# Left window columns weighted by TensorE's diagonals instead of ScalarE, and one block of a third pair added up wholly on TensorE from the eleventh head on

## The chip, the core and the metric

The kernel runs on one core of one Trainium2 chip, in one launch. The metric is the device time in microseconds of one execution; lower is better. The core's engines work side by side and meet only through semaphores: TensorE (PE) multiplies matrices into PSUM, VectorE (DVE) and ScalarE (ACT) work element by element, GpSimd (POOL) issues indirect transfers and small vector work, and SyncE (SP) issues the other transfers.

## The reference, cut to what matters

The input is an image of 4 x 32 x 32 x 384. Layer 0 is a deformable attention with 6 heads of 64 channels; a linear attention and a mixture of experts follow as layer 1. The change touches the attention of layer 0 alone:

```python
attn = jnp.einsum('bmhc,bnhc->bhmn', qh, k) * scale          # 1024 x 1024 per image and head
disp = (ref.reshape(1, n, 1, 2) - pos.reshape(Bq * G, 1, n, 2)) * 0.5
bias = _bilinear_sample(rpe_img, disp)                       # zero border, four neighbours
attn = jax.nn.softmax(attn + bias, axis=-1)
out = jnp.einsum('bhmn,bnhc->bmhc', attn, v).reshape(Bq, Hq, Wq, NC)
```

The bias of one key against all 32 x 32 queries is a 33 x 33 window of a table, interpolated with four weights: an upper and a lower row weight, then a left and a right column weight. With t the window after the row weights, bias[y, x] = w2 * t[y, x] + w3 * t[y, x + 1].

## The kernel before

The attention runs over 24 heads (4 images x 6), which the text counts from 0 to 23. A head has 1024 keys, in 8 blocks of 128, taken as 4 pairs of blocks. There are 96 pairs, numbered p = 4 * head + kp, so the "third pair" of a head is kp = 2. Within a pair the first block is e = 0, the second e = 1. A tile holds the keys of a block on 128 partitions and the 1024 queries along the row; score tiles for a pair are 128 x 2 x 1024.

For each pair these functions run, each on its engine:

- `fetch_windows` (L1168, POOL): one indirect transfer per block brings the 128 windows.
- `upper` (L1184, ScalarE) makes t from the window's upper rows with weight 0; `lower` (L1194, VectorE) adds the lower rows with weight 1. t is 32 rows of 33.
- `left` (L1202, ScalarE) makes o, the left 32 columns of t times weight 2.
- `scores` puts two products into one PSUM tile `ps` for the pair: keys times queries (L1221), and o brought in by a product with the identity (L1226). Each product is cut into 64-row halves, so that q-k products and o products sit on different quarters of the array. A pair has a first and a second half of this work (`step` 0 and 1). Between them stands `turn_over` (L1241): a tiny ScalarE copy of a token, which waits for the first half and which the second half waits for. There is one `ps` buffer, four PSUM banks: the next pair's products start when the last reader of this pair is done.
- `right` (L1252, VectorE), once per block: S = t's right columns times weight 3, plus `ps`.
- `running` (L1270, VectorE) keeps the maximum over the pairs of a head, 128 x 2 x 1024 at a time; after the fourth pair the two halves are joined (L1272). `highest` and `spread` reduce it over the partitions with TensorE transposes (L1282, L1286, L1298) and copy it out of PSUM (L1306, ScalarE).
- `minus` (L1311, VectorE) subtracts the maximum, `weights_of` (L1315, ScalarE) takes exp, `values` (L1329, L1338, TensorE) sums values and weights into PSUM; `out_of` (L1354, ScalarE) copies these sums out after the head's last pair.

A loop over g interleaves pairs at different stages: values of pair g-5, minus and exp of g-4, running maximum of g, scores of g+1, upper, lower and left of g+2, windows of g+4. The order on TensorE, ScalarE, VectorE and POOL is the order in which these calls are written, and each engine's queue is strictly in order. For a head's third pair the calls of one turn stand so: values part 0, scores first half, upper, running, token, values part 1, minus, exp, scores second half, left, right. Remaining work of layer 0 (`project`, L1429 and L1441, and late key and value pieces, L270 and L286) is tucked into fixed places of the loop.

The stage before (convolution, offsets, sampling of x by 6 indirect gathers a tile, L871, and multiplications with VectorE, L886 to L891) is ordered by a planner with costs and due times; the first windows, uppers and lowers of the attention are placed among its last instructions. Tiles come from pools with a set number of buffers; where a pool's memory was another tile's before, the first use waits for that tile's last.

Of the kernel before, what the change touches and what calls it, by code (L numbers as in the profile page):

```python
# [19 lines left out]
P = 128  # L20
# [139 lines left out]
def body(  # L160
# [953 lines left out]

    with tc.tile_pool(name="b_w", bufs=1) as bwp, tc.tile_pool(name="b_qkv", bufs=2) as bq, tc.tile_pool(
        name="b_win", bufs=4
    ) as bwin, tc.tile_pool(name="b_t", bufs=4) as bt, tc.tile_pool(name="b_o", bufs=2) as bo_, tc.tile_pool(
        name="b_s", bufs=6
    ) as bS, tc.tile_pool(name="b_m", bufs=2) as bm, tc.tile_pool(name="b_ao", bufs=1) as bao, tc.tile_pool(
        name="b_y", bufs=3  # L1120
# [2 lines left out]
        nc.sync.dma_start(wo, w_out.rearrange("(a p) d -> p a d", p=P))  # L1123
        bo = bwp.tile([P, NC], F32, tag="bo", name="bo")
        nc.sync.dma_start(bo, bc(b_out, 0, P))
        units = [(b, h) for b in range(B) for h in range(G)]
        ao = {}
        heads = {}
# [28 lines left out]


        wins, ts, os_, pss, Ss, turns = {}, {}, {}, {}, {}, {}
        qk, vs, ms, nms, pbss, pos, avs = {}, {}, {}, {}, {}, {}, {}  # L1160

        def fetch_windows(p):
# [35 lines left out]
        def left(p, e):  # L1198

            if p < NP:  # L1200
                o = bo_.tile([P, HI, WI], F32, tag="o", name=f"o{p}_{e}")
                nc.scalar.activation(o, ts[p, e][:, :, 0:WI], AF.Copy, scale=weight(p, e, 2))  # L1202
                os_[p, e] = o.rearrange("p y x -> p (y x)")

        def scores(p, step):


            if p >= NP:
                return
            i, kp = divmod(p, KP)  # L1210
            if step == 0:
                if kp == 0:
                    qk[i] = load_qk(units[i])
                pss[p] = bps.tile([P, 2, N], F32, tag="s", name=f"ps{p}")
            q, k = qk[i]
            ps = pss[p]
            e, d = 1 - step, step
            made = []
            for f in range(2):
                for r in range(2):  # L1220
                    made.append(nc.tensor.matmul(  # L1221
                        ps[HALF[1 - r], e, FULL[f]], k[HALF[r], 2 * kp + e, :], q[HALF[r], FULL[f]],
                        start=(step == 0), stop=(step == 1),
                    ))
                for r in range(2):
                    made.append(nc.tensor.matmul(  # L1226
                        ps[HALF[r], d, FULL[f]], ident[HALF[r], HALF[r]], os_[p, d][HALF[r], FULL[f]],
                        start=(step == 0), stop=(step == 1),
                    ))
            if step == 0:  # L1230
                turns[p] = made
            else:
                for i_ in made:
                    tc.add_manual_dep(i_.ins, turns[p].ins.name, SYNC, reason="second quarters")
                del turns[p]
# [10 lines left out]
        def right(p):  # L1246

            if p < NP:
                ps = pss.pop(p)
                st = bS.tile([P, 2, N], F32, tag="S", name=f"S{p}")  # L1250
                for e in range(2):
                    nc.vector.scalar_tensor_tensor(  # L1252
                        st[:, e, :].rearrange("p (y x) -> p y x", x=WI),
                        ts.pop((p, e))[:, :, 1:WIN],
                        weight(p, e, 3),
                        ps[:, e, :].rearrange("p (y x) -> p y x", x=WI),
                        ALU.mult,
                        ALU.add,
                    )
                    del os_[p, e]  # L1260
                Ss[p] = st

        def running(p):

            if p < NP:
                i, kp = divmod(p, KP)
                if kp == 1:
                    ms[i] = bm.tile([P, 2, N], F32, tag="m", bufs=1, name=f"m{i}")
                if kp:
                    nc.vector.tensor_tensor(ms[i], Ss[p - 1] if kp == 1 else ms[i], Ss[p], ALU.max)  # L1270
                if kp == KP - 1:
                    nc.vector.tensor_tensor(ms[i][:, 0, :], ms[i][:, 0, :], ms[i][:, 1, :], ALU.max)  # L1272
# [952 lines left out]
```

## Time and profile before

| what | value |
| --- | --- |
| median of 3 runs | 2853.95 us (2847.24 to 2855.77) |
| profiled execution, its own time | 2848.14 us |
| its span, first to last instruction | 2846.1 us |
| TensorE busy, whole span | 2585.0 us (91%) |
| VectorE busy | 1578.6 us (55%) |
| ScalarE busy | 1158.2 us (41%) |
| GpSimd busy | 853.3 us (30%) |
| L1202 (o), ScalarE | 192 instructions, 212.8 us, mean 1144 ns |
| L1226 (o by identity), TensorE | 1536 records, 376.6 us, mean 609 ns |
| L1252 (right), VectorE | 192 instructions, 236.9 us, mean 1275 ns |
| L1270 (running maximum), VectorE | 72 instructions, 172.1 us |
| mean granted TensorE clock | 0.969 |

The busy shares are means over stages with different limits; the attention loop takes about 404 to 1370 us. A row such as L1226 gives the line, engine and operation, what is written and read, how many, their busy time together (overlaps counted once) and the mean of one. Each matrix product of 32-bit numbers appears as two records. "Idle before" is the engine's idle time just before the instruction, and what ended it. In a timeline the columns are start (us), length (us), engine, line, operation, how many were merged, and the idle time.

### The profile page before, as it was taken

Reading aid. Unit: us, or ns where it says so; the run is one execution under the profiler, and the core shown is the slowest. Engines: PE = TensorE matmul, PEld = TensorE weight load, DVE = VectorE, ACT = ScalarE, POOL = GpSimd, SP = SyncE. Lnnn points to the kernel's source line nnn. Section 1 sums busy time; section 2 is a strip of 40 time slices with the busy share of each in tenths; the row PEclk is TensorE's granted clock in tenths of the full one; section 3 lists DMA queues with packets and bytes.
Section 4 is the critical chain, followed back from the end, with each engine's and each line's share of the span. In section 5 each row is a group of like instructions: output and inputs, shape, how many; then the busy total and the mean of one; then the engine's idle time right before and its main releaser. Section 6 shows DMA issues by size and latency. Waiting matters only on the chain. (4 is left out here: it accounts for less than half of the span.)

```text
span 2846.1 us, 33342 instructions
## 1 busy us (share of the span) xinstructions
PE 2585.0 (91%) x12731; PEld 1283.9 (45%) x12731; DVE 1578.6 (55%) x2349; ACT 1158.2 (41%) x1532; POOL 853.3 (30%) x776
## 2 busy tenths in 40 slices
PE   8899838898989988888799898999999999999999
PEld 5555512332333333233365554555555555555566
DVE  3888859999999999999656765000101011011011
ACT  5565536777667766676323322111111111111121
POOL 1668853232333333332112335211112111021121
PEclk9899969999999999999999999999999999999999
DMA  7934575454546555544121312622223434374371
GB/s 205 257 115 133 173 209 165 130 154 145 164 145 194 177 157 149 145 151 127 55 74 52 119 45 70 250 103 103 103 103 119 146 129 142 114 255 172 117 267 58
DMA packets 267899, 404.77 MB, mean 142 GB/s; under 512 B 134674, under 2 KB 207634, under 8 KB 267356
## 3 DMA queue, kind: packets, MB, share of 16 engines
q1 hardware_dynamic: 214912, 230.43, 25.6%
q0 software_dynamic: 52112, 172.15, 18.6%
q8 instruction: 100, 1.64, 0.2%
q14 instruction: 59, 0.48, 0.1%
q10 hardware_dynamic: 716, 0.07, 0.0%
HBM read 345.68 MB, written 70.06 MB: 146 GB/s over the span
## 5 line engine op out<-in xcount | busy, mean ns | idle before, releaser
L2072 PE MATMUL ph<-d_xT,w 128*128 128x512 f32 (+1 forms) x1152 | 484.1, 554 | 1.3 <-ACT h L2079 1.3
L2104 PE MATMUL acc<-w,h 128*128 128x384 f32 x1392 | 480.3, 486 | 0.0
L1168 POOL DMA_INDIRECT win<-table,widx x192 | 278.2, 1449 | 642.4 <-DVE t L1194 612.8
L1221 PE MATMUL ps<-q,k 64*64 64x512 f32 x1536 | 380.3, 608 | 91.6 <-DVE S L1252 43.4
L2079 ACT ACTIVATE h<-ph,b1c 128x512 f32<-128x512 f32 (+1 forms) x192 | 124.2, 647 | 776.2 <-PE ph L2072 761.7
L1226 PE MATMUL ps<-o,ident 64*64 64x512 f32 x1536 | 376.6, 609 | 9.4 <-ACT o L1202 9.4
L2104 PEld LDWEIGHTS acc<-w,h 128*128 128x128 f32 x1392 | 264.1, 190 | 208.5 <-issue 73.2
L2072 PEld LDWEIGHTS ph<-d_xT,w 128*128 128x128 f32 x1152 | 217.0, 191 | 196.3 <-issue 144.5
L871 POOL DMA_INDIRECT ga<-img,pidx x192 | 233.3, 1215 | 145.7 <-DVE gd L600 62.5
L2134 POOL DMA_INDIRECT out<-rows,ei x67 | 67.2, 1003 | 699.4 <-DVE rows L2131 690.5
L1315 ACT ACTIVATE S<-S 128x2048 f32<-128x2048 f32 x96 | 183.4, 1910 | 190.3 <-DVE S L1311 190.3
L1221 PEld LDWEIGHTS ps<-q,k 64*64 64x64 f32 x1536 | 98.8, 133 | 354.4 <-issue 211.3
L1722 DVE COPY d_xT<-e_tr 128x512 f32<-128x512 f32 (+2 forms) x75 | 36.6, 512 | 385.5 <-PE e_tr L1719 385.5
L1194 DVE SCALAR_TENSOR_TENSOR t<-win,bw,t 128x1056 f32<-128x1056 f32 x192 | 244.5, 1314 | 5.1 <-ACT t L1184 3.9
L1252 DVE SCALAR_TENSOR_TENSOR S<-t,bw,ps 128x1024 f32<-128x1024 f32 x192 | 236.9, 1275 | 17.4 <-PE ps L1226 14.3
L2123 DVE SCALAR_TENSOR_TENSOR rows<-b2r,en,rows 128x384 f32<-128x384 f32 x67 | 40.7, 618 | 361.3 <-DMA rows<-out,ei 311.1
L1184 ACT ACTIVATE t<-win,bw 128x1056 f32<-128x1056 f32 x192 | 218.1, 1168 | 40.3 <-DMA win<-table,widx 39.2
L1202 ACT ACTIVATE o<-t,bw 128x1024 f32<-128x1024 f32 x192 | 212.8, 1144 | 35.2 <-DVE t L1194 30.0
L1329 PE MATMUL po<-S,v 128*64 128x512 f32 x768 | 199.0, 642 | 24.4 <-ACT av L1354 13.9
L1311 DVE TENSOR_TENSOR S<-S,pbs 128x2048 f32<-128x2048 f32 x96 | 218.9, 2282 | 2.0 <-ACT pbs L1306 2.0
L2131 DVE SCALAR_TENSOR_TENSOR rows<-acc,en,rows 128x384 f32<-128x384 f32 x67 | 41.4, 618 | 217.6 <-PE acc L2104 215.7
L1270 DVE TENSOR_TENSOR m<-m,S 128x2048 f32<-128x2048 f32 x48 | 117.1, 2440 | 1.6
(350 smaller groups left out, 3441.8 us busy)
## 6 DMA issues: line engine op xcount, KB each, us to landing
w<-in_L_ffn_w SPq DMA_DIRECT2D x50, 2304.0 KB
img<-in_x SPq DMA_DIRECT2D x48, 256.0 KB
q<-q_d SPq DMA_DIRECT2D x48, 256.0 KB
x<-in_x SPq DMA_DIRECT2D x8, 768.0 KB
q_d<-qt SPq DMA_DIRECT2D x24, 256.0 KB
v_d<-qkvw SPq DMA_DIRECT2D x32, 192.0 KB
v<-v_d SPq DMA_DIRECT2D x24, 256.0 KB
k<-k_d SPq DMA_DIRECT2D x48, 128.0 KB
```

The costliest lines, as they stand in the source:

```text
L871: nc.gpsimd.indirect_dma_start(out=ga[:, g].rearrange("p s c -> p (s c)"), out_offset=None, in_=img[b][:, :], in_offset=bass.IndirectOffse ...
L1168: nc.gpsimd.indirect_dma_start(out=win, out_offset=None, in_=tables[h // 2][:, :], in_offset=bass.IndirectOffsetOnAxis(ap=widx[b][:, nb, h ...
L1184: nc.scalar.activation(t.rearrange("p y x -> p (y x)"), wins[p, e][:, : HI * WIN], AF.Copy, scale=weight(p, e, 0),)
L1194: nc.vector.scalar_tensor_tensor(tf, wins.pop((p, e))[:, WIN:], weight(p, e, 1), tf, ALU.mult, ALU.add)
L1202: nc.scalar.activation(o, ts[p, e][:, :, 0:WI], AF.Copy, scale=weight(p, e, 2))
L1221: made.append(nc.tensor.matmul(ps[HALF[1 - r], e, FULL[f]], k[HALF[r], 2 * kp + e, :], q[HALF[r], FULL[f]], start=(step == 0), stop=(step ...
L1226: made.append(nc.tensor.matmul(ps[HALF[r], d, FULL[f]], ident[HALF[r], HALF[r]], os_[p, d][HALF[r], FULL[f]], start=(step == 0), stop=(ste ...
L1252: nc.vector.scalar_tensor_tensor(st[:, e, :].rearrange("p (y x) -> p y x", x=WI), ts.pop((p, e))[:, :, 1:WIN], weight(p, e, 3), ps[:, e, : ...
L1311: nc.vector.tensor_tensor(Ss[p], Ss[p], bc(pbss[p // KP][:, :], 1, 2), ALU.add)
L1329: nc.tensor.matmul(pos[i][0][HALF[f], :], vs[i][:, 2 * kp + e, :], Ss[p][:, e, FULL[f]], start=(first and e == 0), stop=(last and e == 1),)
L2072: nc.tensor.matmul(ph if short(d) else ph[:, :n], a, m, start=(c == 0), stop=(c == CK - 1))
L2104: nc.tensor.matmul(d["acc"][0 if short(d) else s][:, :NC], h[:, s * P : (s + 1) * P], d["w2"][:, hc, :], start=(hc == 0), stop=(hc == HC - 1),
```

## The change

`left` no longer multiplies a block's columns. It makes a 128 x 64 tile: twice the 64 x 64 identity, stacked (`fold`, made once by two GpSimd copies), each row scaled with its key's weight 2. `scores` then multiplies with this diagonal instead of the identity, and moves the left columns of t itself, 16 rows of 32 out of 33, through TensorE.

For the second block of the third pair, in heads 10 to 23 (14 blocks), a second diagonal with weight 3 is made as well, and four further products in the second half of `scores` add the right columns of t to `ps`. `right` then leaves this block out; a ScalarE copy brings it from `ps` into S, and `running` takes the block's maximum out of `ps` directly and the other block's out of S, 128 x 1024 each, in place of one of 128 x 2048. The t pool goes from 4 to 5 buffers, the o pool from 2 to 6 of the smaller tiles.

```diff
@@ -1114,7 +1114,7 @@
 
     with tc.tile_pool(name="b_w", bufs=1) as bwp, tc.tile_pool(name="b_qkv", bufs=2) as bq, tc.tile_pool(
         name="b_win", bufs=4
-    ) as bwin, tc.tile_pool(name="b_t", bufs=4) as bt, tc.tile_pool(name="b_o", bufs=2) as bo_, tc.tile_pool(
+    ) as bwin, tc.tile_pool(name="b_t", bufs=5) as bt, tc.tile_pool(name="b_o", bufs=6) as bo_, tc.tile_pool(
         name="b_s", bufs=6
     ) as bS, tc.tile_pool(name="b_m", bufs=2) as bm, tc.tile_pool(name="b_ao", bufs=1) as bao, tc.tile_pool(
         name="b_y", bufs=3
@@ -1123,6 +1123,12 @@
         nc.sync.dma_start(wo, w_out.rearrange("(a p) d -> p a d", p=P))
         bo = bwp.tile([P, NC], F32, tag="bo", name="bo")
         nc.sync.dma_start(bo, bc(b_out, 0, P))
+
+        fold = bwp.tile([P, GC], F32, tag="fold", name="fold")
+        for e in range(2):
+            nc.gpsimd.tensor_copy(
+                fold[e * GC : (e + 1) * GC, :], ident[e * GC : (e + 1) * GC, e * GC : (e + 1) * GC]
+            )
         units = [(b, h) for b in range(B) for h in range(G)]
         ao = {}
         heads = {}
@@ -1157,6 +1163,8 @@
 
 
         wins, ts, os_, pss, Ss, turns = {}, {}, {}, {}, {}, {}
+
+        WHOLE, rights, direct = ((2, 1),), {}, {}
         qk, vs, ms, nms, pbss, pos, avs = {}, {}, {}, {}, {}, {}, {}
 
         def fetch_windows(p):
@@ -1198,9 +1206,18 @@
         def left(p, e):
 
             if p < NP:
-                o = bo_.tile([P, HI, WI], F32, tag="o", name=f"o{p}_{e}")
-                nc.scalar.activation(o, ts[p, e][:, :, 0:WI], AF.Copy, scale=weight(p, e, 2))
-                os_[p, e] = o.rearrange("p y x -> p (y x)")
+                os_[p, e] = diagonal(p, e, 2)
+                if (p % KP, e) in WHOLE and p // KP >= 10:
+                    rights[p, e] = diagonal(p, e, 3)
+
+        def diagonal(p, e, i):
+            o = bo_.tile([P, GC], F32, tag="o", name=f"o{p}_{e}_{i}")
+            nc.scalar.activation(o, fold, AF.Copy, scale=weight(p, e, i))
+            return o
+
+        def columns_of(p, e, r, f, x0):
+
+            return ts[p, e][HALF[r], 16 * f : 16 * f + 16, x0 : x0 + WI]
 
         def scores(p, step):
 
@@ -1224,8 +1241,13 @@
                     ))
                 for r in range(2):
                     made.append(nc.tensor.matmul(
-                        ps[HALF[r], d, FULL[f]], ident[HALF[r], HALF[r]], os_[p, d][HALF[r], FULL[f]],
-                        start=(step == 0), stop=(step == 1),
+                        ps[HALF[r], d, FULL[f]], os_[p, d][HALF[r], :], columns_of(p, d, r, f, 0),
+                        start=(step == 0), stop=(step == 1 and (p, d) not in rights),
+                    ))
+                for r in range(2 if (p, d) in rights else 0):
+                    made.append(nc.tensor.matmul(
+                        ps[HALF[r], d, FULL[f]], rights[p, d][HALF[r], :], columns_of(p, d, r, f, 1),
+                        start=False, stop=(step == 1),
                     ))
             if step == 0:
                 turns[p] = made
@@ -1248,7 +1270,13 @@
             if p < NP:
                 ps = pss.pop(p)
                 st = bS.tile([P, 2, N], F32, tag="S", name=f"S{p}")
+                whole = None
                 for e in range(2):
+                    if rights.pop((p, e), None) is not None:
+
+                        whole = e
+                        del os_[p, e], ts[p, e]
+                        continue
                     nc.vector.scalar_tensor_tensor(
                         st[:, e, :].rearrange("p (y x) -> p y x", x=WI),
                         ts.pop((p, e))[:, :, 1:WIN],
@@ -1259,6 +1287,9 @@
                     )
                     del os_[p, e]
                 Ss[p] = st
+                if whole is not None:
+                    nc.scalar.copy(st[:, whole, :], ps[:, whole, :])
+                    direct[p] = whole, ps
 
         def running(p):
 
@@ -1266,7 +1297,12 @@
                 i, kp = divmod(p, KP)
                 if kp == 1:
                     ms[i] = bm.tile([P, 2, N], F32, tag="m", bufs=1, name=f"m{i}")
-                if kp:
+                if p in direct:
+
+                    w, ps = direct.pop(p)
+                    for e, of in ((w, ps), (1 - w, Ss[p])):
+                        nc.vector.tensor_tensor(ms[i][:, e, :], ms[i][:, e, :], of[:, e, :], ALU.max)
+                elif kp:
                     nc.vector.tensor_tensor(ms[i], Ss[p - 1] if kp == 1 else ms[i], Ss[p], ALU.max)
                 if kp == KP - 1:
                     nc.vector.tensor_tensor(ms[i][:, 0, :], ms[i][:, 0, :], ms[i][:, 1, :], ALU.max)
```

## The prediction

> **What bounds the kernel now.** I read the page's slices first, to find which engine is full where, then a table of busy time by stretch inside the attention stage, then who VectorE waits for, and last the timeline of one head. Each answers what the one before leaves open.
>
> The slices show a span of 2846.1 us. From slice 6 to slice 18 (about 404 to 1370 us) VectorE stands at 9 tenths and TensorE at 8 or 9. The stretches, of 40 us, separate the two:
>
> ```profile
> core 0: us, PE busy (x) PEld busy (x) DVE busy (x) ACT busy (x) POOL busy (x), PEclk, DMA share, GB/s
> 980.00:1020.00 40.00, 35.59 (x232) 12.66 (x228) 39.63 (x30) 27.44 (x27) 12.33 (x10) 0.96 0.50 155
> 1020.00:1060.00 40.00, 36.93 (x244) 13.31 (x240) 39.63 (x30) 28.44 (x28) 13.75 (x10) 0.96 0.52 154
> ```
>
> VectorE is busy for 39.63 of 40 us. The missing 0.37 us are the slits between 30 instructions. So VectorE sets the pace; TensorE has some 4 us per 40, but that is a mean, and what counts is where those 4 us lie. VectorE's own waits from 440 to 1340 us are only these:
>
> ```profile
> engine line waited for: us in total, times, longest us
> DVE nm L1286 <- PE pm L1282: 10.1, 11, 2.2
> DVE S L1252 <- PE ps L1226: 9.3, 10, 1.3
> ```
>
> Both are waits for TensorE: it is close behind everywhere. How close at the place of the change is in the timeline of the third pair of the seventeenth head (index 16, pair 66). First TensorE, then VectorE, then ScalarE:
>
> ```profile
> 1063.95 1.94 PE L1329 MATMUL po<-S,v 128*64 128x512 f32 x8 [0.27 <-ACT av L1354]
> 1065.82 0.65 PE L1221 MATMUL ps<-q,k 64*64 64x512 f32 x2
> ...
> 1067.70 1.07 PE L1338 MATMUL po<-S,ones 128*32 128x512 f32 x8
> 1068.74 0.65 PE L1221 MATMUL ps<-q,k 64*64 64x512 f32 x2
> 1068.75 0.65 PE L1226 MATMUL ps<-o,ident 64*64 64x512 f32 x2
> 1069.22 0.59 PE L1221 MATMUL ps<-q,k 64*64 64x512 f32 x2
> ...
> 1070.09 0.60 PE L1226 MATMUL ps<-o,ident 64*64 64x512 f32 x2
> ...
> 1059.20 2.29 DVE L1311 TENSOR_TENSOR S<-S,pbs 128x2048 f32<-128x2048 f32 x1
> ...
> 1071.47 2.46 DVE L1252 SCALAR_TENSOR_TENSOR S<-t,bw,ps 128x1024 f32<-128x1024 f32 x2
> 1073.97 2.29 DVE L1270 TENSOR_TENSOR m<-m,S 128x2048 f32<-128x2048 f32 x1
> 1076.17 0.20 DVE L1384 RECIPROCAL ri<-pr 128x8 f32<-128x8 f32 x1
> ...
> 1061.52 1.91 ACT L1315 ACTIVATE S<-S 128x2048 f32<-128x2048 f32 x1 [2.52 <-DVE S L1311]
> 1063.33 1.05 ACT L1354 COPY av<-po 128x512 f32<-128x512 f32 x2
> ...
> 1068.50 0.18 ACT L1241 COPY token<-token 128x1 f32<-128x1 f32 x1
> ```
>
> TensorE's last pass for this pair ends at 1070.69 and VectorE takes the result at 1071.47: 0.78 us of slack. Where VectorE waits, as in head 12, it starts 0.07 us after TensorE's end, so 0.71 us can be used up unseen. The passes show one more thing: the q-k products and the L1226 products of both halves run side by side on four quarters of the array, each product is two records (two passes over its 512 columns), and passes follow each other every 0.43 us.
>
> **The change, part by part.** Durations are those of one profiled execution, 2846.1 us of span within its own time of 2848.14 us. The median of the three runs, 2853.95, lies 5.8 above it; I add my sum to either.
>
> *Left columns on diagonals, all heads.* The 192 ScalarE passes over 128x1024 (L1202, 1144 ns) become 206 of 128x64. The nearest row is ScalarE's 128x48 (L800, 243 ns): I take 0.25 us, bounds 0.2 and 0.38 (128x128 at L2092). That takes 168 us from ScalarE, which is not on the path: it sits idle 12 of 40 us. TensorE's count stays; only the moving operand changes, from a contiguous 512 to 16 rows of 32 out of 33. Zero is my cost for that. The row that bears on it is the convolution, which moves 8 rows of 32 out of 34:
>
> ```profile
> L713 PE MATMUL pcv<-qpad,wc x1728: 373/375/686, 30.0 to 298.1; 64*64 64x256 f32 x192
> ```
>
> A contiguous 128 columns takes 273 ns (L1282) and 512 take 589, so a contiguous 256 would take 378: rows cost nothing there. The Trainium skill speaks against this change in "SBUF — State Buffer", section "Door 1: The DMA port swizzle": SBUF is read in lines of 16 bytes and each step to a new line has a price. Rows 132 bytes apart touch a ninth line three times in four, 9% more lines, which as an estimate would be 0.04 us a pass: eight passes on the path of each head's second pair and twelve of the third, some 14 us in all. I follow the row and keep 14 for the range.
>
> ScalarE's relief gains where its lateness holds TensorE. The second half of a pair waits for the token (L1241). In pairs 18, 26 and 30 the token comes 1.00, 2.06 and 1.00 us after TensorE's first half, and VectorE then waits 0.25, 1.00 and 0.24 us. These 1.5 us go. Elsewhere the token is 0.1 us late, or 0.74 in most third pairs, but there the sums of L1338 stand between the halves and allow a start only 0.04 us sooner.
>
> *The extra products.* In 14 heads (index 10 to 23) the second block of the third pair gets four more products, on quarters that L1226's products already occupy. Two column halves times two passes times 0.43 us make 1.72 us more before the pair is finished, whatever the other quarters do meanwhile. The changed program's list of waits has VectorE's first addition (L1280 there) wait for the last of them. Could TensorE start sooner? No: the pair's chain hangs on VectorE's L1311, which ends at 1061.49; ScalarE's exp (1.91) and av (1.05) follow, then TensorE's 1063.95 and 1065.82. None of that is shortened. So of 1.72 us, 0.71 + 0.04 are covered and 0.97 become a VectorE wait. I measured the slack in all 14 heads: nine have 0.78 or 0.79 (9 x 0.97 = 8.7); head 18 has 0.32 (1.72 - 0.25 - 0.04 = 1.43); head 23 0.55 (1.20); heads 12, 13 and 19 have none, VectorE waits there already, so 1.72 each, less 0.30 in head 12 for a late token (1.42 + 1.72 + 1.72). Sum: 16.2 us.
>
> *VectorE's own exchange.* Removed: one addition (half of 1071.47 to 1073.97, 1.25) and the 128x2048 maximum (1073.97 to 1076.17, 2.20), 3.45 us. Added: a 128x1024 maximum out of PSUM, 1.25 like the addition that reads PSUM, and one out of SBUF (L1272, 1.14 from start to start): 2.39. That would be 1.06 us gained per head. But the new ScalarE copy of the whole block stands between: in the list of waits the copy waits for VectorE's first addition, and the PSUM maximum waits for the copy. No run shows this copy; its nearest row is L1306, 128x1024 out of PSUM, 993 ns. With 0.03 us from VectorE to ScalarE (1061.49 to 1061.52) and 0.10 back (401.59 to 401.69, as L1194 follows L1184), VectorE idles 1.12. Net +0.05 per head, +0.7 us. The trace of before holds no case of two engines reading one `ps`. The skill's "PSUM — Partial Sum Buffer", section "PSUM bank collisions raise a hardware error", says that no two engines may touch one bank and quadrant at once, readers included, which is a reason for such waits. Without them the sum would be 1.12 x 14 = 15.7 us better; I go by the waits.
>
> Queued behind the copy on ScalarE are the two L1184 of the next-but-one pair. They start near 1074.8 instead of 1073.02 and are needed by VectorE near 1080.2: covered. The fourth pair's products start about 2.1 us later (PSUM comes free after the PSUM maximum) while VectorE comes 1.03 later; slacks of 1.3 to 2.8 us there shrink by about 1.1 and hold.
>
> *The start.* Other pool sizes move addresses, so the first three table windows now stand on POOL ahead of the last 24 gathers, ScalarE's first L1184 ahead of a key copy, VectorE's first L1194 behind an earlier multiplication, and a new `fold` copy on POOL waits for the last gathers before the fourth window. Windows land 5.6 us after issue (median), so near 366 us; ScalarE's key and value copies (348 to 361) slip to about 380, SP's table, v, q and k transfers, which wait for them, by about 12 us, and the second k lands near 405 instead of 393. VectorE's first L1252 then comes at 411 to 415 instead of 412.07. I take +1.5, bounds -3 and +6.
>
> Sum: 16.2 + 0.7 - 1.5 + 1.5 = +16.9 us: 2848.14 becomes 2865.0, the median 2853.95 becomes 2870.9.
>
> **The rivals.** *TensorE has room* (no change): the extra 1.72 us fit, because with ScalarE relieved the third pair runs earlier. For it: the token was 0.74 late. Against: the sums between the halves. It would leave 0.7 - 1.5 + 1.5 = +0.7, so 2854.7. *The copy is off the path* (faster): one mechanism, at VectorE's PSUM maximum: if it did not idle for the copy, 1.12 us come back per head, 15.7 in all, and to end below by 0.3% the extra products must in addition find at least 0.7 us per head of earlier start; it decides once the two together exceed 1.8 us a head: about 2839. The list of waits speaks against it. *Rows are dear* (slower still): the 9% above, 16.9 + 14 = 2885. *The start slips further*: q and k land later than 405, up to 2877.
>
> **How the numbers follow.** About 0.3%, 8.6 us, is what a measurement of this kernel can tell from no change. Forecast 0.66; room on TensorE, whole or nearly, 0.15; faster 0.05; dear rows 0.07; late start 0.07. Faster 0.05, same 0.15, slower 0.80. The forecast's own range is 2862 to 2878; taking in half of the no-change case and the dearer ones short of their ends gives 2856 to 2881.
>
> **What would show it.** Right: waits of VectorE's L1280 for TensorE of about 1 us in 14 third pairs; just after each, 1.1 us idle before the PSUM maximum, put down to ScalarE's copy; heads from 10 on about 41.2 us long instead of 40.2, heads before that unchanged; ScalarE's busy time down by about 150 us; L1243 at 589 ns. Wrong: third pairs with no such wait, L1243 above 600 ns, heads below 10 that change their length, or a first L1280 outside 409 to 418 us.

## The result, and the profile after

The changed kernel takes 2880.28 us (median of 4 executions, 2876.68 to 2884.0) where the kernel before takes 2854.86 on the same chip (4 executions, 2847.24 to 2855.97): ratio 1.0094, 95% interval 1.0077 to 1.0111, or 25.4 us more. The profiled execution took 2876.68 us with a span of 2875.0. The forecast was 2870.9, that is 16.9 us more: the direction came and so did the third pairs, but the sum was 8.5 us too small. A second measurement beside other kernels (e16) gave 1.0072, 1.0058 to 1.0087, 22.8 us more.

A stretch of the attention stage first, one head further on than before because everything lies later:

```profile
core 0: us, PE busy (x) PEld busy (x) DVE busy (x) ACT busy (x) POOL busy (x), PEclk, DMA share, GB/s
996.00:1036.00 40.00, 36.48 (x237) 12.52 (x236) 38.17 (x29) 20.96 (x29) 12.93 (x10) 0.96 0.54 158
```

VectorE was busy 39.63 of 40 us; now 38.17. ScalarE fell from 27.44 to 20.96. What VectorE does in the rest is in its list of waits from 440 to 1340 us, which had two rows before:

```profile
DVE m L1304 <- ACT S L1291: 14.7, 13, 1.1
DVE S L1280 <- PE ps L1248: 13.5, 13, 2.9
DVE S L1280 <- PE ps L1243: 11.6, 25, 2.0
DVE nm L1322 <- PE pm L1318: 11.6, 11, 2.2
```

The first two rows are new, one for each half of the change in the third pairs: the maximum out of PSUM waits for ScalarE's copy, and the addition waits for the extra products (L1248). The same pair as before, head 16's third (TensorE, VectorE, ScalarE):

```profile
1086.46 1.02 PE L1243 MATMUL ps<-t,o 64*64 64x512 f32 x4
1087.32 1.02 PE L1248 MATMUL ps<-t,o 64*64 64x512 f32 x4
1088.39 1.28 DVE L1280 SCALAR_TENSOR_TENSOR S<-t,bw,ps 128x1024 f32<-128x1024 f32 x1 [0.56 <-PE ps L1248]
1090.80 1.22 DVE L1304 TENSOR_TENSOR m<-m,ps 128x1024 f32<-128x1024 f32 x1 [1.13 <-ACT S L1291]
1089.76 1.01 ACT L1291 COPY S<-ps 128x1024 f32<-128x1024 f32 x1 [1.96 <-DVE S L1280]
```

TensorE's last pass ends at 1088.34 and VectorE starts at 1088.39: the slack of 0.78 us is gone and 0.56 us of idling stands in its place. Then 1.13 us more for the copy. The rows of the new operations:

```profile
L1243 PE MATMUL ps<-t,o 64*64 64x512 f32 x1536 | 382.6, 614 | 2.7 <-ACT o L1215 2.7
L1215 ACT ACTIVATE o<-fold,bw 128x64 f32<-128x64 f32 x206 | 58.8, 338 | 26.5 <-POOL fold L1129 26.5
```

The strided product costs what the contiguous one did (614 to 609 ns). The 26.5 us of L1215 are one single idle time, in the stage's start, and they lead to the part that the forecast missed:

```profile
408.62 0.23 POOL L1129 COPY fold<-ident 64x64 f32<-64x64 f32 x1 [6.26 <-DMA ga<-img,pidx]
409.30 0.98 POOL L1176 DMA_INDIRECT win<-table,widx  x1 [0.44 <-POOL fold L1129]
```

GpSimd's second `fold` copy waits 6.26 us for the last gather, and the fourth window's fetch stands behind it: issued at 409.30, where before it was issued at 397.38:

```profile
397.38 0.93 POOL L1168 DMA_INDIRECT win<-table,widx  x1 [0.30 <-issue]
```

ScalarE waits for `fold` as well. VectorE's first addition then comes at 418.74 instead of 412.07 (first the kernel before, then the changed one):

```profile
412.07 2.47 DVE L1252 SCALAR_TENSOR_TENSOR S<-t,bw,ps 128x1024 f32<-128x1024 f32 x2 [0.64 <-PE ps L1226]
418.74 2.47 DVE L1280 SCALAR_TENSOR_TENSOR S<-t,bw,ps 128x1024 f32<-128x1024 f32 x2
```

Meanwhile TensorE's granted clock has dropped; between 420 and 430 us the column PEclk, third from the end, reads 1.00 in the kernel before:

```profile
420.00:430.00 10.00, 7.03 (x42) 2.08 (x38) 9.47 (x7) 7.57 (x8) 2.70 (x2) 1.00 0.37 115
```

and 0.52 in the changed one:

```profile
420.00:430.00 10.00, 8.00 (x33) 2.17 (x34) 4.23 (x5) 2.92 (x5) 2.70 (x2) 0.52 0.62 204
```

To place the 28.8 us by which the two spans differ, I subtract, pair by pair, the start of VectorE's first addition of a right column (called R below; R0 is that of pair 0):

| stretch | before | after | difference |
| --- | --- | --- | --- |
| start to R0 | 412.07 | 418.74 | +6.7 (3.1 of it are there at 76 us, ahead of every reordered instruction) |
| R0 to R5 | 42.94 | 47.47 | +4.5 |
| R5 to R40 (heads 1 to 9) | 356.43 | 353.44 | -3.0 |
| R40 to R95 (heads 10 to 23) | 549.95 | 566.56 | +16.6 |
| R95 to the end | 1484.73 | 1488.74 | +4.0 |

These are single executions, and that of the kernel before was a quick one (2848.14 us, where the median is 2854.86). The first row overstates the change for that reason; e17 below shows by how much.

### The profile page after: what moved, and what is told of

Its sections match the earlier page's. It is cut to its first block, busy times and chain, and to the rows that moved or that the text cites. A ratio compares the mean times of both kernels' runs of the same rounds, so it can differ in the third digit from the quotient of the medians.

```text
span 2875.0 us, 33410 instructions
## 1 busy us (share of the span) xinstructions
PE 2619.6 (91%) x12843; PEld 1296.8 (45%) x12843; DVE 1563.5 (54%) x2349; ACT 1017.8 (35%) x1560; POOL 884.5 (31%) x778
## 3 DMA queue, kind: packets, MB, share of 16 engines
q1 hardware_dynamic: 214912, 230.43, 25.4%
## 5 line engine op out<-in xcount | busy, mean ns | idle before, releaser
L1176 POOL DMA_INDIRECT win<-table,widx x192 | 307.0, 1599 | 624.2 <-DVE t L1202 593.9
L1243 PE MATMUL ps<-t,o 64*64 64x512 f32 x1536 | 382.6, 614 | 2.7 <-ACT o L1215 2.7
L1280 DVE SCALAR_TENSOR_TENSOR S<-t,bw,ps 128x1024 f32<-128x1024 f32 x178 | 220.2, 1274 | 34.4 <-PE ps L1243 19.6
L1891 POOL DMA_INDIRECT tab_d<-ent,si x64 | 65.5, 1024 | 163.5 <-DVE selw L1886 140.9
L713 PE MATMUL pcv<-qpad,wc 64*64 64x256 f32 x1728 | 104.4, 392 | 5.0 <-ACT oT L725 5.0
```

The costliest lines, as they stand in the source:

```text
L1176: nc.gpsimd.indirect_dma_start(out=win, out_offset=None, in_=tables[h // 2][:, :], in_offset=bass.IndirectOffsetOnAxis(ap=widx[b][:, nb, h ...
L1243: made.append(nc.tensor.matmul(ps[HALF[r], d, FULL[f]], os_[p, d][HALF[r], :], columns_of(p, d, r, f, 0), start=(step == 0), stop=(step == ...
L1280: nc.vector.scalar_tensor_tensor(st[:, e, :].rearrange("p (y x) -> p y x", x=WI), ts.pop((p, e))[:, :, 1:WIN], weight(p, e, 3), ps[:, e, : ...
```

## The experiments

The runs fell on several chips of two kinds. On those of e9 to e18 the kernel before takes 2852 to 2857 us; on those of e1 to e8 it takes 2915 to 2917, single executions of it lie some 40 us apart, so that intervals are wide there, and the stage before attention ends some 60 us later. The stretch R40 to R95 hardly depends on the chip (549.95 and 550.06 us for the kernel before, 549.6 to 551.4 in all eight traces without whole blocks), so the third pairs are read from it. My theory: TensorE's extra products and ScalarE's copy, both on VectorE's path in fourteen third pairs, and a disturbed start. The rivals: dear strided rows, or diagonals that cost in every head; a start that was one execution's accident.

### Third pairs: e2, e3, e9, e10

**e2**, ScalarE's copy behind the maximum:

```diff
                 if whole is not None:
-                    nc.scalar.copy(st[:, whole, :], ps[:, whole, :])
                     direct[p] = whole, ps
...
                     for e, of in ((w, ps), (1 - w, Ss[p])):
                         nc.vector.tensor_tensor(ms[i][:, e, :], ms[i][:, e, :], of[:, e, :], ALU.max)
+                    nc.scalar.copy(Ss[p][:, w, :], ps[:, w, :])
```

> The changed kernel with one line moved: ScalarE's copy of the block finished on TensorE is issued after VectorE's maximum out of PSUM, not before it. All products and copies stay. Theory (in each of the fourteen third pairs VectorE idles 1.13 us before the maximum for the ScalarE copy, beside the wait for the longer chain of products): 14 x 1.1 = 15.7 us less, some 2864.5 us, ratio 1.0034; the wait of m for ScalarE's S is gone. Rival (the products' 1.7 us on the chain set the cadence, so that the time given back at the maximum comes back as a longer wait for the next scores): under 4 us gained, ratio above 1.0075, with VectorE's waits for ps in the pair after longer by about 1 us each.

2932.57 us against 2916.64, ratio 1.0054 (1.0024 to 1.0083), which says little on a chip of this kind. R40 to R95 says more: 559.4 us, 6 to 7 less than in the changed kernel (565.0 and 566.6), not 15.7. The wait of the maximum is gone, as the theory had it, but a good half of it returns. In most even heads nothing comes back. In the odd ones VectorE waits 0.46 us before the fourth pair's addition, and in most of these it waits again at the reduction of the transposed maximum, because the transposes L1318 stand on TensorE behind the next head's scores (head 15):

```profile
1122.88 1.23 DVE L1322 TENSOR_REDUCE nm<-pm 128x8 f32<-128x1024 f32 x1 [0.99 <-PE pm L1318]
```

Together 0.46 + 0.99 over two heads is 0.72 a head, and 1.13 - 0.72 = 0.41, times 14 is 5.7 us. TensorE follows so closely that this gain on VectorE was worth under half of itself.

**e3**, no whole blocks:

```diff
-        WHOLE, rights, direct = ((2, 1),), {}, {}
+        WHOLE, rights, direct = (), {}, {}
```

> The changed kernel without the whole blocks: no extra products, no copy, no maximum out of PSUM; left columns on diagonals in all heads, buffers as in the changed kernel. Theory (the fourteen third pairs cost 16.6 us, the start 8, the diagonals themselves gain some 3): 16.6 us less than the changed kernel, some 2863.5 us, ratio 1.003. Rival (matmuls that read rows of 32 out of 33 elements, or the small matrices, slow every head): ratio above 1.007.

2917.48 us against 2916.64: ratio 1.0007 (0.9977 to 1.0036), and 550.9 us from R40 to R95. All but 1 us of the 16.6 in heads 10 to 23 belongs to the whole blocks; matmuls that read rows of 32 out of 33 cost nothing that shows.

**e9**, the products for the right columns left out, copy and split maximum kept:

```diff
-                for r in range(2 if (p, d) in rights else 0):
+                for r in range(0):
```

> The changed kernel without the products for the right columns (L1248): the right columns of the fourteen blocks are left out, while ScalarE's copy and VectorE's two half maxima stay. To be read by the stretch from the first addition of pair 40 to that of pair 95, which takes 550.0 us in the kernel before on either chip and 565.0 to 566.6 us in the changed one. Theory (the products on the chain into VectorE cost the 15 to 16 us; the exchange with its wait for ScalarE's copy is neutral): 550 to 552 us, no wait before the first addition of a third pair (0.56 us in the changed kernel), the wait for the copy still 1.13 us. Rival (the wait for ScalarE's copy is the cost): 560 us or more.

2865.37 us against 2852.41, ratio 1.0038 (1.0023 to 1.0052); 554.5 us from R40 to R95. VectorE's waits from 812 to 1340 us:

```profile
DVE m L1304 <- ACT S L1291: 14.7, 13, 1.1
DVE S L1280 <- PE ps L1243: 7.2, 16, 1.2
```

The wait for the copy stands in full, yet 12 of the 16.6 us are gone: the products are the cost. The exchange with its wait pays for itself where it stands (from a third pair's R to the fourth's is 0.03 us shorter than in the kernel before). The 4.5 us that stay are more than the 0 to 2 expected. In nine of the heads the first maximum takes 2.45 us where it took 2.29, 1.5 us together; all traces with five buffers of t have that, e3 too, and none with four. So it stands in head 16, first the kernel before, then the changed one:

```profile
1064.13 2.29 DVE L1270 TENSOR_TENSOR m<-S,S 128x2048 f32<-128x2048 f32 x1
1080.26 2.45 DVE L1306 TENSOR_TENSOR m<-S,S 128x2048 f32<-128x2048 f32 x1
```

Head 18's third pair makes 1.2; traces without any diagonal (e6, e13, e17) have as much there. Three pairs that are not third ones, ahead of the additions of pairs 48, 52 and 95, make 2.5, and small gains elsewhere take some back.

**e10**, these products twice:

```diff
-                    made.append(nc.tensor.matmul(
+                    for again in range(2):
+                        made.append(nc.tensor.matmul(
```

> The changed kernel with each product for the right columns (L1248) issued twice, so that the right columns of the fourteen blocks count double. Theory (every product on this chain is paid in full once the slack is used up): 14 x 1.72 = 24 us more in the stretch from pair 40 to pair 95, 589 to 591 us, and VectorE's wait before a third pair's addition 2.3 us instead of 0.56. Rival (TensorE's four quarters hide the products, and something else makes the wait): under 575 us.

2904.19 us against 2852.41, ratio 1.0172 (1.0156 to 1.0187); R40 to R95 takes 591.2 us, 24.7 more than in the changed kernel, and the wait before a third pair's addition is 2.31 us. Four products more make 1.76 us more per head: here, past the slack, they are paid in full, although other quarters of the array work beside them.

### The start: e1, e5 to e7, e13, e14, e16 to e18

**e1**, the changed kernel with four buffers of t and with later buffers at their old addresses. The order of the instructions at the start is then that of the kernel before, and the two `fold` copies stand 24 gathers earlier:

```diff
-    ) as bwin, tc.tile_pool(name="b_t", bufs=5) as bt, ...
+    ) as bwin, tc.tile_pool(name="b_t", bufs=4) as bt, ...
...
-        fold = bwp.tile([P, GC], F32, tag="fold", name="fold")
+        bo_.tile([P, 2048 - 7 * GC], F32, tag="pad", name="pad", bufs=1)
+        fold = bo_.tile([P, GC], F32, tag="fold", name="fold", bufs=1)
```

> The changed kernel with one thing put back: the buffers of the pools b_t and b_o and the small matrix fold lie so that every later buffer has the address that it had in the kernel before (b_t has four buffers again; fold and a pad stand inside b_o's old 8192 bytes). The first window fetches then stand behind the last gathers on GpSimd again. Theory (about 8 us of the 25 are lost in the stage's start, because the moved addresses let window fetches and copies go ahead of the last gathers, and TensorE then starts the first heads cold): 8 us less than the changed kernel, some 2872 us, ratio to the kernel before 1.006; last gather multiplication (L886) back near 399 us from 414, first VectorE addition of a right column (L1280) near 412 us. Rival (the late start is the run's own accident, or the diagonals are what costs in the first heads): no change, ratio 1.009, and the first addition stays near 419 us. Second rival (four buffers of t instead of five cost more than the start gains): above 1.009.

2927.26 us against 2916.64, ratio 1.004 (1.0009 to 1.0072): undecided, since the changed kernel itself gives 1.0047 (1.0022 to 1.0072) on a chip of this kind (e7). The marks at 399 and 412 us that I had named can't be used here, where the stage before ends some 60 us later.

**e5, e6, e7**, together on such a chip: the kernel before again, the kernel before with `fold` alone, the changed kernel again. The edit of e6:

```diff
         nc.sync.dma_start(bo, bc(b_out, 0, P))
+        fold = bwp.tile([P, GC], F32, tag="fold", name="fold")
+        for e in range(2):
+            nc.gpsimd.tensor_copy(
+                fold[e * GC : (e + 1) * GC, :], ident[e * GC : (e + 1) * GC, e * GC : (e + 1) * GC]
+            )
```

> The kernel before, unchanged, for a profile on the same chip as the three beside it, and to show what the measurement makes of no change: ratio 1.000, within 0.002 on a steady chip.

> The kernel before with the small matrix fold alone: 256 bytes more in the pool b_w and its two copies on GpSimd; nothing reads it. Every later buffer lies 256 bytes further on. That alone puts the first three window fetches ahead of the last 24 gathers on GpSimd and puts upper halves and left columns ahead of key copies on ScalarE, as in the changed kernel. Theory (the moved addresses cost the start): 4 to 8 us slower than the kernel before, ratio 1.0014 to 1.0028, with 4 to 8 us more between the last gather's issue (L871) or a mark ahead of it and the first addition of a right column; all later pairs as in the kernel before. Rival (the changed kernel's late start was that run's own accident): ratio 1.000 within 0.001.

> The changed kernel again on this chip, to compare with the others of this call: ratio 1.009 within 0.002 by its first measurement; heads 10 to 23 longer by 16 to 17 us than in the kernel before on this chip, the start by 4 to 11 us.

e5: 2914.5 against 2915.18, 0.9989 (0.9961 to 1.0018): no change reads as none. e6: 2927.25, ratio 1.0032 (1.0008 to 1.0055). Two copies that nobody reads cost 12 us (2 to 16 by the interval; 4 to 8 were expected). In the traces e6 lies 1.1 us behind e5 at 411 us and 12.1 behind at pair 5, and stays 12.3 behind to pair 95; R40 to R95 is 549.98. e7: 2930.82, 1.0047, below the 1.009 expected; its heads 10 to 23 take 565.0 us, 15.0 more than e5's where 16 to 17 were expected, and its start from 411 us to pair 5 costs 6.8 us.

**e13, e14 and e16**, on a chip of the steadier kind, side by side: e6's, e1's and the changed kernel again.

> The kernel before with the unread 256 bytes of fold alone, again. Theory (the start's order, 11 to 12 us by the first run's trace and medians): ratio 1.004 within 0.001. Rival (the start costs only the 2 to 3 us of the later fold copy, the rest was that run's): under 1.0015.

> The changed kernel with the addresses as in the kernel before, again. Theory (start given back, third pairs kept): 5 to 9 us less than the changed kernel in this call; by its own traces the stretch of heads 10 to 23 is 2 us longer in it, so that 3 to 7 us show. Rival (addresses are worth nothing in the changed kernel): equal within 2 us.

> The changed kernel, for the comparison within this call: ratio 1.009 within 0.002 on a chip that runs the kernel before in 2855 us, 1.005 to 1.007 on one that runs it in 2915 us.

| kernel | median us | ratio to 2854.14 | 95% interval |
| --- | --- | --- | --- |
| e13, before with `fold` alone | 2863.5 | 1.0029 | 1.0017 to 1.0041 |
| e14, changed, old addresses | 2867.43 | 1.0042 | 1.0029 to 1.0056 |
| e16, changed | 2876.96 | 1.0072 | 1.0058 to 1.0087 |

Added alone, the disturbance costs 9.4 us (4.9 to 11.7); taken away, it gives 9.5 back. That is not one execution's accident. But the 9.5 is not all in the start: of the traces of e14 and e16, 3.8 us apart in all, e16 is 2.7 us behind at R5, loses 4.1 more behind R95, and gains 3.1 between them.

**e17 and e18** ask which part of it. e17 is the kernel before with the 256 bytes in the pool and no copies:

```diff
         nc.sync.dma_start(bo, bc(b_out, 0, P))
+        bwp.tile([P, GC], F32, tag="fold", name="fold")
```

e18 is the changed kernel with the copies on VectorE:

```diff
-            nc.gpsimd.tensor_copy(
+            nc.vector.tensor_copy(
```

> The kernel before with 256 unread bytes in the pool b_w and no copies: window fetches, upper halves and left columns stand in the order of e13, but GpSimd has no fold copy. Theory A (the fold copy's wait on GpSimd is most of the start's cost): within 3 us of the kernel before, ratio under 1.001; fourth window issued about 1.3 us after the last gather. Theory B (three windows ahead of the gathers are the cost: 1.67 MB on full DMA engines): 6 to 9 us, ratio 1.002 to 1.003, with the last gather multiplication as late as in e13 (407 us).

> The changed kernel with the two fold copies on VectorE, among the last gather multiplications. Theory A: 6 to 9 us less than the changed kernel, ratio 1.005 to 1.006. Theory B: within 3 us of the changed kernel, ratio 1.007 to 1.009.

e17: 2856.14 against 2856.55, ratio 1.0004 (0.9994 to 1.0014). The three windows ahead of the gathers, with all that they carry along on ScalarE and VectorE, cost nothing that can be measured (the interval runs from -1.7 to +4.0 us). The fourth window's fetch behind the copies, in the timeline of e13:

```profile
407.72 1.83 POOL L1128 COPY fold<-ident 64x64 f32<-64x64 f32 x1 [6.64 <-DMA ga<-img,pidx]
409.81 0.98 POOL L1173 DMA_INDIRECT win<-table,widx  x1 [0.27 <-POOL fold L1128]
```

and in e17, where no copy stands ahead of it:

```profile
402.08 1.50 POOL L1169 DMA_INDIRECT win<-table,widx  x1 [0.30 <-issue]
```

The delay reaches R0 through VectorE's queue: the lower half made from this fourth window (L1199 in e13, L1195 in e17) is queued ahead of the first addition (L1257, L1253). First e13, then e17:

```profile
417.88 1.32 DVE L1199 SCALAR_TENSOR_TENSOR t<-win,bw,t 128x1056 f32<-128x1056 f32 x1 [8.44 <-ACT t L1189]
421.74 2.47 DVE L1257 SCALAR_TENSOR_TENSOR S<-t,bw,ps 128x1024 f32<-128x1024 f32 x2 [1.01 <-PE ps L1231]
413.85 1.32 DVE L1195 SCALAR_TENSOR_TENSOR t<-win,bw,t 128x1056 f32<-128x1056 f32 x1 [2.13 <-ACT t L1185]
417.71 2.47 DVE L1253 SCALAR_TENSOR_TENSOR S<-t,bw,ps 128x1024 f32<-128x1024 f32 x2 [1.01 <-DMA xk<-in_x]
```

So e13 is 4.0 us later at R0, and R0 to R5 takes 46.99 us against 43.02, another 4.0; every later stretch agrees within 0.4 us. These two traces also correct the table of the result: e17's R0, at 417.71, is 5.6 us behind the 412.07 of the kernel before, although its median is no higher; 3.3 of it are there at 353 us, ahead of VectorE's first reordered instruction. Most of the first row's +6.7 goes with the quick execution of the kernel before, not with the change.

e18 is less clear: 2872.23 against 2856.55, ratio 1.0064 (1.005 to 1.0079), between the two expectations. R0 comes at 414.5 instead of 417.1 to 420.4 (four traces with the changed kernel's start on chips of this kind), but R0 to R5 takes 47.25 us, with PEclk at 0.69 from 420 to 430 us. So in the kernel before the GpSimd copy is the whole price that can be measured. In the changed kernel moving it brought no clear gain: in this trace 2.6 us or more at R0, and a longer stretch to R5 at a lower clock. What lowers the clock there stays open.

### Other places for the gain: e4, e8, e11, e12, e15

**e8 and e15**: diagonals in all heads, no whole blocks, old addresses (the edits of e1 and e3 together).

> Left columns on diagonals in all heads, no whole blocks, and addresses as in the kernel before. Theory (the diagonals lift the waits for late tokens in pairs 14, 18, 26 and 30, some 3 us together, and cost nothing): 3 us less than the kernel before, ratio 0.999. Rival (the strided reads or the smaller matrices cost in every head): above 1.002.

> Diagonals in all heads, no whole blocks, addresses as in the kernel before, again. Theory (3.3 us gained in pairs 14, 18, 26 and 30, up to 1.7 us lost in the first five pairs, nothing later): 1.5 to 3.5 us less than the kernel before, ratio 0.9988 to 0.9995. Rival (nothing gained): 1.000 or above.

2911.33 against 2915.18, 0.9988 (0.9961 to 1.0015), and 2853.89 against 2854.14, 0.9992 (0.9982 to 1.0002). In the traces R5 to R40 is 3.3 and 1.6 us shorter than the kernel before's 356.4 to 356.5: both have 1.7 us less in pairs 18, 26 and 30, and e8 alone has 1.35 less in pair 14, though the kernels are the same. With the whole blocks on top (e14) the median is 13.5 us higher and R40 to R95 17.4 longer in the traces (568.5 against 551.1). The diagonals alone are the best version found; that they are faster than the kernel before is not established (1.5 to 3.5 us had been expected of e15).

**e4**: the edits of e1 and e2 together.

> Both edits: addresses as in the kernel before, and ScalarE's copy behind VectorE's maximum. Theory (start 8, bubble 15.7, both additive): some 2856 us, ratio 1.0005, between 0.998 and 1.003. Rival (chain of products sets the cadence): 1.004 or more.

2928.49 against 2916.64, ratio 1.0025 (0.9995 to 1.0056), with 561.1 us from R40 to R95: the copy's 1.13 us does not come back whole here either.

**e11**, the whole block in the fourth pair, with the edits of e4:

```diff
-        WHOLE, rights, direct = ((2, 1),), {}, {}
+        WHOLE, rights, direct = ((3, 1),), {}, {}
```

> The block that is whole on TensorE is taken from the fourth pair, not from the third; ScalarE's copy behind the maximum; addresses as in the kernel before. The chain of scores of a fourth pair ends 1.27 to 2.78 us ahead of VectorE's addition in the kernel before (0.8 us in a third pair), so that 1.72 us of products are covered in half of the heads and wait 0.45 us in the other half. Theory: VectorE saves 1.07 us a head and gives 0.2 back, 14 x 0.85 = 12 us less than in the kernel before between pair 40 and pair 95, 538 us; with the diagonals' 3 us some 2840 us on a chip that runs the kernel before in 2855, ratio 0.995. Rival (the transposes of the maximum, which follow the fourth pair on TensorE, come as late as VectorE comes early): 548 us or more, ratio 0.999 or above.

2865.38 against 2852.41, ratio 1.0038 (1.0026 to 1.005); R40 to R95 takes 561.8 us, not 538. The products are covered as computed or better (mostly waits of 0.20 us, in one head of two), and the rival that I had named takes more than all of it. From 812 to 1340 us VectorE waits 25.0 us, twelve times, for the transposes of the maximum, where the kernel before waits 2.5:

```profile
1059.89 1.23 DVE L1323 TENSOR_REDUCE nm<-pm 128x8 f32<-128x1024 f32 x1 [1.85 <-PE pm L1319]
```

**e12**, the whole block in the first pair, with the edit of e1; ScalarE's copy stands right behind VectorE's addition:

```diff
-        WHOLE, rights, direct = ((2, 1),), {}, {}
+        WHOLE, rights, direct = ((0, 1),), {}, {}
...
-                    direct[p] = whole, ps
```

> The whole block is taken from the first pair, whose scores end 4.7 to 5.9 us ahead of VectorE's addition; ScalarE copies it from PSUM behind VectorE's addition of the other block, and no maximum reads PSUM; addresses as in the kernel before. Theory (products cost only what the pair's slack does not cover; but the second pair's scores start only when the copy has read PSUM, 2.3 us after the addition's start instead of 2.5, so that what VectorE saves it waits before the second pair's addition): nothing lost and nearly nothing gained, 548 to 551 us between pair 40 and pair 95, VectorE's wait before a second pair's addition up from 0.14 to some 1.3 us. Rival (extra products cost their 1.7 us a head wherever they stand): 565 us or more. Second rival (the second pair's chain starts with the shorter addition): 535 us.

2884.47 against 2852.41, ratio 1.0102 (1.0086 to 1.0117); R40 to R95 takes 577.1 us. None of my theories: the products are hidden, VectorE does not wait for scores in the second pair at all, and yet 27 us are lost. ScalarE's line and VectorE's line tell why:

```profile
1075.15 1.01 ACT L1292 COPY S<-ps 128x1024 f32<-128x1024 f32 x1 [3.59 <-DVE S L1281]
1077.27 2.55 DVE L1203 SCALAR_TENSOR_TENSOR t<-win,bw,t 128x1056 f32<-128x1056 f32 x2 [2.23 <-ACT t L1193]
```

ScalarE stands 3.59 us in front of the copy, until VectorE's addition is done; the upper halves L1193, queued behind the copy, come late, and VectorE waits 2.23 us for them: 29.0 us in thirteen waits up to 1340 us. The transposes of the maximum take another 18.1 us there, where the kernel before waits 2.5; what VectorE saves on its additions makes up for some of it.

## Why the prediction was right, and where it was not

The step that failed is the start, priced at +1.5 us: what was measured for it alone is 9.4. A smaller one is the stretch behind the attention loop, which the sum did not have at all. The third pairs, the main term, were right in their mechanism and nearly so in their sum.

*Extra products, +16.2, and VectorE's exchange, +0.7.* Right: 16.6 us in heads 10 to 23 against 16.9, and 15.0 in e7's trace. In every third pair the finish moved from 1.95 us after the second half's start to 3.66, by 1.72 as was worked out; VectorE's idle time for the copy is 1.13 where 1.12 was. The stall itself is smaller than computed, 0.56 us and not 0.97, because the slack is larger with five buffers of t: 1.14 us in e3, which has no whole blocks, and not 0.78 (e15, with four buffers, has 0.81, and e14 a stall of 0.88). Of the difference 0.16 is the head's first maximum, which brings VectorE later to the third pair; the rest is TensorE's, whose chain starts earlier. From one third pair's R to the next a usual head is 0.8 us longer, not 1.0. Heads 12, 13 and 18, with 1.4, 1.7 and 2.85 in the third pair, and three pairs that are not third ones, with 2.5 together, make up the difference; head 19, for which 1.72 was set down, has none. That the sum came so near is in part luck: heads 18 and 19 alone differ by 1.6 us each between two traces of the changed kernel. e9 and e10 show that the products carry it: 12.0 us less without them, 24.7 more with twice as many.

*Strided rows, 0.* Right. The Trainium skill's "SBUF — State Buffer", section "Door 1: The DMA port swizzle", would have made 14 us, as an estimate, of the 16-byte lines that rows 132 bytes apart touch; L1243 takes 614 ns against 609, single passes 0.59 to 0.60 us as before. Heads 10 to 23 take 0.9 and 1.1 us longer in e3 and e15, but 1.2 and 1.4 longer in e17 and e13, which have no diagonals. The measurement decides: rows of this stride show no price here.

*Late tokens, -1.5.* Right: pairs 18, 26 and 30 gave 0.31, 1.08 and 0.31 us, 1.7 together, in every trace with diagonals. Pair 14 gave another 1.35 in the changed kernel, which makes the -3.0 of the table; but this is no late token, because e13 and e17 have 0.93 of it without diagonals, and e14 and e15 none with them. What makes it stays open.

*The start, +1.5, bounds -3 and +6.* This is the step that failed: 9.4 us added alone (e13), and up to 9.5 taken away (e14). I had all its parts in the text and priced the wrong ones. The three windows ahead of the gathers, on which I worked out arrivals to the microsecond, cost nothing that can be measured (e17). The `fold` copy, of which I wrote only that it waits for the last gathers, holds GpSimd's queue, and behind it the fourth window is issued 12 us later than in the kernel before (7.7 later in e13 than in e17). And the sum ended at the first addition: a lower clock of TensorE in the next five pairs was not in it. R0 to R5 is 4.5 us longer in the first trace, 2.2 in e16's.

*Behind the loop, not in the sum.* From R95 to the end is 4.0 us longer in the first trace of the changed kernel and 6.8 in e16's, with the granted clock of the last section beside it.

With 9.5 for 1.5, and 1.7 for 1.5 at the tokens, the sum is 16.9 + 8.0 - 0.2 = 24.7 us, between the two measurements of 22.8 and 25.4. This is a sum of medians; as the traces of e14 and e16 show, some of the 9.5 belongs behind the loop.

*The signs of being wrong.* Three of those named came up. The first L1280, at 418.74, is outside 409 to 418 us; but e16's, at 417.12, is inside, so this mark is too fine for one execution. Heads below 10 changed their length, by the 3.0 us above. L1243 is above 600 ns, but L1226 had 609 already: this mark was set wrong, on the length of a single pass. ScalarE's busy time fell by 140 us, where about 150 was named.

*The rival "the copy is off the path"* asked what would happen if VectorE did not idle for it. e2 made that case: 6 to 7 us, not 15.7. Where a second engine follows at some tenths of a microsecond, as here, an idle time that is removed is not a gain of its length.

## What to carry to other kernels

A new small instruction is priced by its place in its queue, not by its length: ask what it waits for, and what stands behind it. Two copies of 64 x 64 on GpSimd, with nobody reading their result, cost 9 us because a window's fetch was queued behind their wait for a last gather; in the trace 4 us of it are the delay itself, and 4 the longer pairs right after it, at a lower clock. And where two engines run with tenths of a microsecond between them, work moved from one to the other is free only up to the slack of the very pair in which it lands, and what it saves on the first engine is capped by the second engine's next wait.

## What the hardware showed that I had not expected

TensorE's granted clock is part of a stage's start. While the last gathers land, from 30 to 10 us ahead of R0, PEclk is 0.50 in all twenty traces. In the kernel before it is at 1.00 from 420 to 430 us; in the changed kernel it is at 0.52 there, and pair 1's second half takes 3.69 us instead of 1.95. R0 to R5 is 42.9 to 43.0 us in five traces (the kernel before twice, e14, e15, e17) and 44.6 to 47.5 in the other fifteen. Read in stretches of 5 us from 10 to 30 us behind R0, PEclk is 1.00 throughout in the five, and falls to 0.50 to 0.80 in each of the fifteen. The order of instructions alone does not decide it: e1, e4, e8, e11 and e12 start in the order of e14 and e15, and take 44.6 to 46.9 us.

The same happens behind the stage. From 36 to 44 us after R95 PEclk is 1.00 in twelve traces, and 0.50 to 0.82 in eight; in these eight the part from R95 to the end takes 1490.9 to 1494.5 us, in the others 1482.5 to 1488.7. Seven of the eight are among the eight traces with five buffers of t (the changed kernel's first trace is the one without it); the eighth, e6, is one of twelve with four. What decides it is not shown; the Trainium skill ("TensorE: Matmul & The Clock Gate", section "What's actually happening") has the activity watched in free-running windows of about 3.4 us, which would let the same gap halve the clock in one execution and not in the next, but no run here shows the windows. It is worth some 6 us, and the difference between 22.8 and 25.4 us, or between two traces of one kernel, is smaller than that.
